# Last image's sums and norms spread by matrix products, x kept in its frame, squares summed by contiguous quarters

## The chip, the cores and the metric

One core of a Trainium2 chip runs the whole program, once, for a batch of 32 images. The metric is the device time in microseconds; runs of the kernel before took 4459.23, 4460.05 and 4460.9 us.

## The reference

The input is 32 images of 128 channels by 64 x 64 positions (T = 4096 tokens of 128 channels), all in float32. Cut to what matters:

```python
# layer 0
x = x + conv(group_norm(x))                  # 3x3 kernels mixed per image by a softmax over 4
# layer 1
t = tokens(x)
t = t + attn(ln_t(t))
t = t + ffn(ln_t(t))
return from_tokens(t)

def attn(x):
    xb  = x @ w_down.T + b_down              # 128 -> 16
    att = windowed_attention(xb)             # 4 heads of 4, windows of 144 tokens at stride 72:
                                             # softmax(q k / 2) v, overlaps added, divided by counts
    out = x + sigmoid(gate) * (att @ w_up.T + b_up)
    return layer_norm(out) * ln_gamma + ln_beta
def ffn(x):
    wx = x @ W.T; wx = batch_norm(wx)        # over all images and tokens
    y_t = sigmoid(wx_t + y_{t-1} @ V.T)      # a scan over the tokens
    return y
```

Three norms over the 128 channels of each token matter here: `ln_t` before the attention (called k = 0 in the kernel), the attention's own layer norm (k = 1), and `ln_t` before the ffn (k = 2). Channels lie on partitions, so the mean and the sum of squares of a token are sums over partitions, and 1/deviation must be brought back to all partitions.

## The kernel before, in words

The program has two stages. `images()` handles the 32 images (b = 0 to 31) as jobs that overlap; `by_runs()` then does the ffn's scan in four streams of two-image groups, which needs the batch norm's statistics of all images and so cannot start before the last image is done.

**Jobs and order.** Each image has thirteen generators (line 1386 on): `load` (statistics, kernel mix), `taps`, `waves`, `conv`, `drain` (a Winograd-like convolution, two halves of 32 rows), `project` (k = 0 norm and projection), `feed`, `values`, `attend` (21 score steps: 7 blocks of windows times 3), `divide0` and `divide1` (softmax denominators, output projection, in two halves of blocks 0 to 3 and 4 to 6), `tail` (k = 1 norm, output x) and `last` (k = 2 norm, ffn input z). Each yields a step: engine, a pool for a result tile, what it reads and writes. A planner that runs when the program is built keeps a model of the five engines (`Clock`), takes the step that can start earliest in the model, and breaks ties by a priority of job and progress from the table `DUE`:

```python
a, w, n = DUE.get(job[0], (-1.0, 0.0, 1))
key = at, job[1] + a + w * job[4] / n - (9 if len(job[3]) > 4 else 0)
```

So each engine's instructions stand in one fixed order, which the table sets. Where the model sees PE idle for over 0.6 us, it puts filler products in (`nm<-fWc`, the constants `SPARE`).

**Tiles.** PSUM: three banks `nms`, one per product of nearly all jobs, given back when the result is read; one four-bank tile `scs` for the scores and for the output projection `wc`; one bank `av` for the weighted values. SBUF: two image frames `xs` (66 x 66 positions, the second stage's first group reuses them as `framed`), three big tiles `zt`, five buffers `places`.

**The norms.** `deviations(src, b, k, mean)` squares the source in four strided parts on ACT into a `place`, sums each over the partitions on PE into one `nm` tile (with the mean beside it for k = 0 and 2), copies that to SBUF, moves it by small DMAs to a tile `cp` of 128 partitions by 32 tokens, takes 1/deviation there (`inv_dev`: exp of -ln/2 and a Newton step), and stores it to `r_d` in DRAM. `spread` then loads each quarter of 1024 tokens from `r_d` to all partitions (512 KB) and multiplies on DVE. In `tail` a second set of loads brings x back from `x_d`, where `project` had stored it.

**The softmax sums.** In `attend` the sums of the exponentials come out as four extra rows in each group of 32 of `av`, copied to `avs` block by block. `divide` moves these rows to `cd` by DMA, takes reciprocals, stores them to `s_d`, loads them spread over the rows, multiplies, loads the mean from `r_d` into row 16 (so that the product with `wc` also subtracts it), and does the products with `wc` and the additions into `zt`.

**The end.** `by_runs` begins with the batch norm's sums (line 1865 on), then loads the z of the next groups. Its group 0 is read from `framed`, which holds the z of images 0 and 1; both were loaded when image 31's k = 0 norm had been applied.

Nearly all instructions of the first stage carry line 243, the planner's recording wrapper, so they are told apart by tile names: `nm`, `sc`, `av` in PSUM, `frames` for `xs`, `place`, `cp`, `cd`, `avs`, `zt`. Parts of names after `<-` are what an instruction reads.

Of the kernel before, what the change touches and what calls it, by code (L numbers as in the profile page):

```python
# [8 lines left out]
F32 = mybir.dt.float32  # L9
AF = mybir.ActivationFunctionType  # L10
ALU = mybir.AluOpType
# [31 lines left out]
    "setup": (0.44, 0.04, 8),  # L43
    "load": (-0.91, 0.63, 29),
    "taps": (0.04, 0.16, 6),
    "waves": (-0.12, 0.52, 26),
# [3 lines left out]
    "feed": (1.63, 0.54, 27),  # L50
    "values": (1.44, 1.24, 28),
    "attend": (1.24, 1.1, 71),
    "divide0": (1.88, 0.1, 15),
    "divide1": (2.21, 0.02, 11),
    "tail": (2.42, 0.75, 33),
    "last": (2.99, 0.86, 40),
# [202 lines left out]
def hybrid_kernel(  # L259
# [60 lines left out]
    )  # L320
    grp = const.tile([P, 32, 4], F32, name="grp")
# [96 lines left out]
    def images(nc):  # L418
# [6 lines left out]
        with ExitStack() as pa:  # L425
# [88 lines left out]
            def deviations(src, b, k, mean):  # L514

                dims = "p (c r y) w -> p r c y w" if k == 0 else "p (c r t) -> p r c t"
                parts = src.rearrange(dims, c=4, r=4)
                for r in range(4):
                    buf = yield from place("ACT", (src,))
                    sq = units(buf)  # L520
                    nc.scalar.activation(
                        sq if k else sq.rearrange("p c (y w) -> p c y w", w=W), parts[:, r], AF.Square
                    )
                    if r == 0:
                        yield "PE", nms, (sq, parts[:, :, :])
                        ps = clock.take("PE", nms)
                    else:
                        yield "PE", None, (sq,)
                    if mean and r == 0:
                        for i in range(4):  # L530
                            for c in range(4):
                                nc.tensor.matmul(
                                    ps[32 * c : 32 * c + 32, UNIT : 2 * UNIT],
                                    avg[:, 32 - i : 64 - i],
                                    parts[:, i, c],
                                    start=(i == 0),
                                    stop=(i == 3),
                                )
                    for c in range(4):
                        nc.tensor.matmul(  # L540
                            ps[32 * c : 32 * c + 32, 0:UNIT],
# [303 lines left out]
            def project(b):  # L845
# [19 lines left out]
                if b == NB - 1:  # L865

                    while ("tail", NI - 1) not in done:
                        yield
# [1269 lines left out]
```

## Time and profile before

| | |
|---|---|
| three runs, median | 4460.05 us (4459.23 to 4460.9) |
| the profiled execution | 4460.42 us, its span 4458.6 us |
| PE busy | 4180.4 us, 94% |
| DVE busy | 3554.4 us, 80% |
| ACT busy | 2410.3 us, 54% |
| POOL busy | 1691.4 us, 38% |
| first stage ends (last `bn_aggr` of image 31) | 3908.6 us |
| mean granted PE clock | 0.975 |

Times in the answers are microseconds from the start of the span. A row of the timeline has start, length, engine, line, operation, tile written, tiles read, shapes and count; in brackets the idle time of the engine before it and what ended that. An fp32 product shows as two PE rows. SPq is the queue of SP, which issues the DMAs; the length of its row is the issue, not the transfer.

### The profile page before, as it was taken

The page shows a single profiled execution, that of the slowest core. Times are in us where ns is not written, and L with a number is a line of the kernel's source. Part 1 is how long each engine was busy: PE and PEld are TensorE (multiplying, and loading weights), DVE is VectorE, ACT ScalarE, POOL GpSimd, SP SyncE. Part 2 cuts the span into 40 slices and gives each one's busy share as a digit, 9 for nine tenths or more (in the row PEclk, how much of TensorE's full clock was granted, in tenths as well). Part 3 has the DMA queues.
Part 4 walks back from the last instruction along what each step waited for, and adds up shares of the span by engine and source line. Part 5 has one row for each costly group of instructions (what it writes and reads, how often), then busy time and mean ns, then how long its engine had stood idle before and what let it go on. Part 6 is the DMA issues. An engine that isn't in the chain of part 4 may idle for free.

```text
span 4458.6 us, 103741 instructions
## 1 busy us (share of the span) xinstructions
PE 4180.4 (94%) x42729; PEld 2191.2 (49%) x42729; DVE 3554.4 (80%) x5364; ACT 2410.3 (54%) x3500; POOL 1691.4 (38%) x1652
## 2 busy tenths in 40 slices
PE   5999999999999999999999999999999998689987
PEld 2544444555455455455455455455455455455443
DVE  7778787888788888888888888888888864459884
ACT  1445555555555555555555555555555565257774
POOL 3443333334334333333333333333333322037765
PEclk9999999999999999999999999999999999899998
DMA  3434554555555555555555555555555544549998
GB/s 105 135 107 168 167 174 146 185 183 174 183 176 172 177 181 177 175 183 164 182 184 171 164 186 168 174 180 172 169 182 179 176 150 148 180 202 264 283 263 171
DMA packets 467575, 789.44 MB, mean 177 GB/s; under 512 B 338048, under 2 KB 348304, under 8 KB 434320
## 3 DMA queue, kind: packets, MB, share of 16 engines
q1 hardware_dynamic: 456480, 715.38, 49.0%
q0 software_dynamic: 8704, 67.11, 7.3%
q8 instruction: 339, 5.55, 0.5%
q14 instruction: 148, 1.21, 0.1%
q10 hardware_dynamic: 1904, 0.18, 0.0%
HBM read 499.06 MB, written 276.76 MB: 174 GB/s over the span
## 4 chain that ended last, share of the span: by engine, by line
PE 61%; DVE 20%; DMA 9%; issue 4%; ACT 2%; SPq 2%; POOL 1%; DVEq 0%; ACTq 0%; POOLq 0%
PE nm L243 33%; PE sc L243 13%; PE av L243 10%; DVE zt L243 6%; PE v L1968 3%; DVE v L1974 3%; DVE frames L243 2%; DMA zr<-z_d 2%; DVE cp L243 2%; SPq L243 2%; ACT ex L243 2%; DMA out_dram<-zr 2%; DVE h L243 1%; DVE st L243 1%; DMA place<-x_d 1%
## 5 line engine op out<-in xcount | busy, mean ns | idle before, releaser
L243 ACT ACTIVATE ex<-sc 128x1728 f32<-128x1728 f32 x672 | 1082.1, 1610 | 825.3 <-PE sc L243 792.9
L243 POOL TENSOR_TENSOR qe<-qs,mqk 128x576 f32<-128x576 f32 x448 | 615.8, 1378 | 1025.1 <-PE sc L243 1020.9
L243 PE MATMUL nm<-u,w 128*128 128x512 f32 x1536 | 785.5, 631 | 19.0 <-POOL w L243 18.9
L243 PE MATMUL sc<-qe,ks 32*128 32x432 f32 (+1 forms) x7168 | 669.6, 443 | 41.9 <-POOL qe L243 21.6
L243 PE MATMUL av<-ex,VE 128*32 128x144 f32 x14336 | 624.6, 292 | 5.7 <-DVE avs L243 5.4
L243 PEld LDWEIGHTS av<-ex,VE 128*32 128x32 f32 x14336 | 390.3, 110 | 313.9 <-issue 244.2
L243 PEld LDWEIGHTS sc<-qe,ks 32*128 32x128 f32 x7168 | 286.2, 185 | 431.0 <-issue 172.1
L1968 PE MATMUL v<-yw,fVT 128*128 128x254 f32 (+1 forms) x1504 | 438.3, 429 | 35.3 <-ACT yw L1981 25.6
L1979 ACT ACTIVATE yw<-v,shf 128x254 f32<-128x254 f32 (+1 forms) x752 | 353.8, 473 | 123.4 <-DVE v L1974 48.2
L1974 DVE SCALAR_TENSOR_TENSOR v<-zr,scl,v 128x256 f32<-128x256 f32 (+1 forms) x585 | 347.5, 662 | 90.5 <-PE v L1968 90.4
L243 PEld LDWEIGHTS nm<-u,w 128*128 128x128 f32 x1536 | 266.3, 194 | 307.4 <-issue 271.7
L243 POOL TENSOR_TENSOR u<-frames 128x528 f32<-128x528 f32 x256 | 392.8, 1544 | 37.1 <-PE nm L243 34.5
L243 PE MATMUL nm<-u,h 128*128 128x512 f32 x768 | 383.4, 618 | 0.0
L1968 PEld LDWEIGHTS v<-yw,fVT 128*128 128x128 f32 x1504 | 242.0, 195 | 244.3 <-ACT yw L1979 194.2
L243 ACT ACTIVATE place<-zt 128x1024 f32<-128x1024 f32 x256 | 259.8, 1050 | 175.9 <-DVE zt L243 166.6
L243 DVE SCALAR_TENSOR_TENSOR u<-u,u 128x528 f32<-128x528 f32 x256 | 246.4, 974 | 58.0 <-POOL u L243 56.5
L1985 POOL COPY zr<-yw 128x256 f32<-128x256 f32 x416 | 257.7, 730 | 85.6 <-ACT yw L1979 84.6
L243 PE MATMUL nm<-zt,fWc 128*128 128x512 f32 x512 | 276.2, 638 | 14.3 <-ACT zt L243 14.2
L243 PE MATMUL nm<-place,avg 128*32 128x256 f32 x3072 | 236.3, 390 | 6.4 <-ACT place L243 6.4
L243 DVE SCALAR_TENSOR_TENSOR zt<-sc,gbk,zt 128x576 f32<-128x576 f32 (+1 forms) x192 | 174.5, 909 | 70.0 <-PE sc L243 69.0
L243 DVE TENSOR_TENSOR zt<-frames,place 128x1024 f32<-128x1024 f32 x128 | 211.5, 1682 | 21.2 <-DMA place<-r_d 21.2
L243 ACT COPY zt<-nm 128x512 f32<-128x512 f32 x256 | 149.1, 584 | 141.0 <-PE nm L243 139.7
(205 smaller groups left out, 6262.7 us busy)
## 6 DMA issues: line engine op xcount, KB each, us to landing
place<-r_d SPq DMA_DIRECT2D x384, 512.0 KB
place<-in_conv_k_dram SPq DMA_DIRECT2D x128, 576.0 KB
x_d<-frames SPq DMA_DIRECT2D x32, 2112.0 KB
place<-x_d SPq DMA_DIRECT2D x128, 528.0 KB
frames<-in_x_dram SPq DMA_DIRECT2D x128, 512.0 KB
out_dram<-zt SPq DMA_DIRECT2D x64, 1024.0 KB
z_d<-zt SPq DMA_DIRECT2D x64, 1024.0 KB
zr<-z_d SPq DMA_DIRECT2D x26, 2048.0 KB
```

What stands on the lines that cost most here:

```text
L243: got = f(*args, **kw)
L1968: nc.tensor.matmul(self.ps[:, :, c], fVT, self.yw[1 - r % 2][:, :, c], start=not whole, stop=True)
L1974: nc.vector.scalar_tensor_tensor(v, z, scl, v, ALU.mult, ALU.add)
L1979: nc.scalar.activation(y[:, :, c], self.ps[:, :, c], AF.Sigmoid, bias=shf)
L1985: nc.gpsimd.tensor_copy(z, y)
```

## The change

For all images, `deviations` takes four contiguous quarters of 1024 tokens, not four strided parts, and each quarter waits only for a gate of its own: for k = 0 the half of the convolution that writes its rows, for k = 2 that quarter of `tail`'s result. The `nm` tile is taken at the first quarter. For the last image alone:

- 1/deviation for k = 1 and 2 is taken on the PSUM sums directly, 128 partitions by 256 tokens (`inv_dev` into a `place`), and `beam` spreads it to all partitions by four products of 32 rows for each quarter, into halves of `scs`; DVE multiplies from PSUM.
- `finish` replaces `divide0` and `divide1`: after each block it spreads the sums by a product with a selector, takes reciprocals of 128 x 288 on DVE and multiplies; the output projection (`added`, split from `divide`) follows after blocks 3 and 6. The mean of k = 0 is subtracted in `project` (`less`).
- x is not stored to `x_d`: ACT adds `bet` to it in its frame, and `tail` adds it from there. Of the first group's z, only the other frame's image is loaded early; this frame's is loaded after `tail` has read x.
- `last` writes its product to a tile of its own, `zw`, so both halves of the product can come ahead of the spread.

The table `DUE` has new values for most jobs. The diff, cut:

```diff
 DUE = {
-    "setup": (0.44, 0.04, 8),
+    "setup": (-0.16, 0.04, 8),
     "load": (-0.91, 0.63, 29),
-    "taps": (0.04, 0.16, 6),
-    "waves": (-0.12, 0.52, 26),
+    "taps": (0.02, 0.22, 6),
+    "waves": (-0.25, 0.4, 26),
     "conv": (-0.45, 1.09, 36),
...
-    "feed": (1.63, 0.54, 27),
+    "feed": (1.72, 0.61, 27),
     "values": (1.44, 1.24, 28),
-    "attend": (1.24, 1.1, 71),
-    "divide0": (1.88, 0.1, 15),
-    "divide1": (2.21, 0.02, 11),
-    "tail": (2.42, 0.75, 33),
-    "last": (2.99, 0.86, 40),
+    "attend": (1.15, 1.27, 71),
+    "divide0": (1.92, 0.02, 15),
+    "divide1": (2.34, 0.02, 11),
+    "tail": (2.39, 0.56, 33),
+    "last": (2.96, 0.89, 40),
 }
...
+            def deviations(src, b, k, mean, gate):
+
+                dims = "p (g j) (v t) -> p j v g t" if k == 0 else "p (g j v t) -> p j v g t"
+                for c in range(4):
+                    while gate(c) not in done:
+                        yield
+                    quart = src[:, 16 * c : 16 * c + 16] if k == 0 else src[:, quarter(c)]
+                    buf = yield from place("ACT", (quart,))
...
+                    nc.scalar.activation(lines(buf[:, 0:QT]) if k == 0 else buf[:, 0:QT], quart, AF.Square)
+                    if c == 0:
+                        yield "PE", nms, (buf[:, 0:QT], quart)
                         ps = clock.take("PE", nms)
...
+                if b == NB - 1 and k:
+                    buf = yield from place("ACT", (ps,))
+                    v, l, dst = (buf[:, UNIT * i : UNIT * (i + 1)] for i in range(3))
+                    if mean:
+                        nc.scalar.activation(l, ps[:, UNIT : 2 * UNIT], AF.Square)
+                        yield "DVE", None, (l, ps), (v,)
+                        nc.vector.tensor_max(v, ps[:, 0:UNIT], l)
+                        nc.vector.tensor_sub(v, v, l)
+                    else:
+                        v = ps[:, 0:UNIT]
+                    yield from inv_dev(dst, v, l)
+                    nms.append(ps)
+                    return buf, dst
...
-                nc.sync.dma_start(
-                    r_d[b, k, n - 2 : 2].rearrange("k (p t) -> p k t", t=32), cp[:, n:4]
-                )
+                for i in range(n, 4):
+                    nc.sync.dma_start(
+                        r_d[b, k, i - 2].rearrange("(g r t) -> r g t", r=4, t=32), cp[:, i]
+                    )
...
+            def beam(got, use):
+
+                buf, dev = got
+
+                def cast(c):
+                    for r in range(4):
+                        nc.tensor.matmul(
+                            ps[:, r, UNIT * (c % 2) : UNIT * (c % 2 + 1)],
+                            once[32 * r : 32 * r + 32, c : c + 1].to_broadcast([32, P]),
+                            dev[32 * r : 32 * r + 32],
+                            start=True,
+                            stop=True,
+                        )
+
+                yield "PE", scs, (dev,)
+                ps = clock.take("PE", scs)
+                cast(0)
+                for c in range(4):
+                    if c < 3:
+                        yield "PE", None, (dev,), (ps[:, :, UNIT * ((c + 1) % 2) : UNIT * ((c + 1) % 2 + 1)],)
+                        cast(c + 1)
+                    yield "DVE", None, (ps,), ()
+                    use(c, ps[:, :, UNIT * (c % 2) : UNIT * (c % 2 + 1)].rearrange("p r (g t) -> p r g t", t=32))
+                scs.append(ps)
+                spare.append(buf)
...
                             nc.vector.scalar_tensor_tensor(y[3], tl, 8.0, y[3], ALU.mult, ALU.add)
+                    done["rows", b, 2 * i] = done["rows", b, 2 * i + 1] = True
...
-                yield "SP", None, (rows(xt, 0, H),)
-                nc.sync.dma_start(x_d[b], xt[:, 1 : H + 1])
-                yield from deviations(rows(xt, 0, H), b, 0, True)
+                if b < NB - 1:
+                    yield "SP", None, (rows(xt, 0, H),)
+                    nc.sync.dma_start(x_d[b], xt[:, 1 : H + 1])
+                yield from deviations(rows(xt, 0, H), b, 0, True, lambda c: ("rows", b, c))
...
+                    yield from spread(less(i) for i in range(4))
+                    yield "ACT", None, (), (rows(xt, 0, H),)
+                    nc.scalar.activation(rows(xt, 0, H), rows(xt, 0, H), AF.Identity, bias=bet)
                     while ("tail", NI - 1) not in done:
                         yield
                     yield "SP", None, ()
-                    for i in range(NI):
-                        nc.sync.dma_start(framed[:, i], z_d[i])
+                    i = (b + 1) % NI
+                    nc.sync.dma_start(framed[:, i], z_d[i])
...
+            def finish(b):
...
+                for m in range(NWG):
+                    while ("block", b, m) not in done:
+                        yield
+                    t = slice(2 * WIN * m, 2 * WIN * (m + 1))
+                    yield "PE", nms, (av[:, t], sel[:, 0:P])
+                    ps = clock.take("PE", nms)
+                    nc.tensor.matmul(ps[:, 0 : 2 * WIN], sel[:, 0:P], av[:, t], start=True, stop=True)
+                    yield "DVE", None, (ps,), (av[:, t], rc)
+                    nc.vector.reciprocal(rc, ps[:, 0 : 2 * WIN])
+                    nc.vector.tensor_mul(av[:, t], av[:, t], rc)
+                    nms.append(ps)
+                    if m in (3, NWG - 1):
+                        yield from added(b, m // 4, zt, DK)
+                spare.append(sel)
...
+                def straight(i, w):
+                    z = zt[:, quarter(i)]
+                    zu = z.rearrange("p (g r t) -> p r g t", r=4, t=32)
+                    nc.vector.tensor_mul(zu, zu, w)
+                    nc.vector.scalar_tensor_tensor(
+                        lines(z), lines(z), gam, rows(xs[b % NF], 16 * i, 16), ALU.mult, ALU.add
+                    )
+                    done["x2", b, i] = True
+
+                got = yield from deviations(zt[:, 0:T], b, 1, False, lambda c: ("div", b, 1))
+                if b < NB - 1:
+                    yield from spread(second(i, k) for i in range(4) for k in range(2))
+                else:
+                    yield from beam(got, straight)
+                    yield "SP", None, (rows(xs[b % NF], 0, H),)
+                    nc.sync.dma_start(framed[:, b % NI], z_d[b % NI])
...
+                got = yield from deviations(zt[:, 0:T], b, 2, True, lambda c: ("x2", b, c))
                 st = sml.tile([P, NBLK, 6], F32, name="st3")
+                zw = zt
+                if b == NB - 1:
+                    zw = big.tile([P, T + 8], F32, name="zt")
+                    for h in range(2):
+                        yield from product(h)
+                    yield from beam(got, straight)
```

## The prediction

> **What bounds the kernel now.** I read the busy times by stage first, then the drain in order of time, then its waits. Stages (stretch in us, its length, then busy us of PE, PEld, DVE, ACT, POOL with instructions, granted PE clock, DMA share, GB/s):
>
> ```profile
> 1000.00:2000.00 1000.00, 973.25 (x11000) 499.51 (x10992) 838.71 (x1224) 545.54 (x724) 362.20 (x291) 0.99 0.56 177
> 2000.00:3000.00 1000.00, 975.95 (x10982) 503.97 (x10984) 848.04 (x1230) 552.25 (x740) 373.68 (x297) 0.99 0.55 175
> ...
> 3728.00:3798.00 70.00, 65.23 (x992) 40.58 (x992) 28.38 (x43) 44.72 (x50) 13.76 (x12) 1.00 0.33 105
> 3798.00:3838.00 40.00, 28.30 (x212) 17.65 (x204) 21.61 (x33) 7.75 (x12) 0.00 (x0) 0.83 0.41 144
> 3838.00:3870.00 32.00, 25.57 (x190) 18.95 (x190) 20.48 (x25) 6.48 (x11) 0.00 (x0) 0.87 0.72 265
> 3870.00:3909.00 39.00, 15.38 (x74) 6.37 (x74) 11.98 (x21) 10.69 (x16) 0.00 (x0) 0.68 0.36 126
> ```
>
> In the steady part PE is busy 97%; 35 us of each 1000 are filler products (`nm<-fWc`, 242 of them in 2000 to 3000). The 32 stores of x to `x_d` start from 89.3 to 3624.5, so an image takes 3535.2/31 = 114.0 us, of which PE has 2.9 idle and 4.0 of filler: 6.9 us of slack. DVE is next, at 84%. From 3798.2, where the last image's attention ends, to 3908.6, where its last `bn_aggr` ends, 110.4 us pass in which no engine is the bound; half of PE's rows are filler. What the time is spent on, in order of time:
>
> ```profile
> 3812.82 0.33 SPq L243 DMA_DIRECT2D s_d<-cd  x1
> ...
> 3821.46 1.06 DVE L243 TENSOR_TENSOR avs<-avs,place 128x864 f32<-128x864 f32 x1 [8.67 <-DMA place<-s_d]
> ...
> 3829.41 1.82 PE L243 MATMUL sc<-avs,wc 17*128 17x432 f32 x8
> ...
> 3877.36 5.36 SPq L243 DMA_DIRECT2D cp<-place  x8
> 3883.96 0.64 DVE L243 TENSOR_TENSOR cp<-cp 128x32 f32<-128x32 f32 x3 [13.54 <-DMA cp<-place]
> ...
> 3886.14 0.33 SPq L243 DMA_DIRECT2D r_d<-cp  x1
> ...
> 3891.66 1.23 DVE L243 TENSOR_TENSOR zt<-zt,place 128x1024 f32<-128x1024 f32 x1 [5.54 <-DMA place<-r_d]
> ...
> 3903.22 1.23 DVE L243 TENSOR_TENSOR zt<-zt,place 128x1024 f32<-128x1024 f32 x1 [6.57 <-DMA place<-r_d]
> ```
>
> Each spread of a small result over the partitions is a chain of transfers: 6.6 us from the issue of `cp<-place` to its first reader, 5.5 from `r_d<-cp` to the first quarter that uses it, and 31 us from the last attention product to the first `wc` product of the second half.
>
> **The last image, step by step** (times are of this execution, 3798.2 onwards; where an operation has no row, the nearest is scaled).
>
> *Softmax sums.* `finish` replaces both `divide(31, d)`: their `cd`, `s_d`, `place` and `avs` transfers go. Added per block: one 128x288 product, a reciprocal and a multiplication. Reciprocals take 0.82 us at 108 and 1.04 at 144 columns, 6.0 ns a column, so 1.9 at 288; the product scales from 128x432 (two rows of 0.54) to 0.7; copy and multiplication 0.45 each. Six of the seven blocks lie in the stretch 3728 to 3798, where DVE is 41% busy: their 6 x 2.4 = 14 us are hidden there; with the cover gone they would cost that. Queued on DVE behind a waiting reciprocal are the spread multiplications of image 30. The last block is on the path: with hops 3.9 us. The selector needs two POOL copies (0.7 us at 256 columns by `zr<-yw`, POOL 20% busy there) and keeps one of five `place` buffers through the attention: nothing while image 30 needs three.
> The four `wc` steps of the first half come out of the transfers' shadow: they now use the one `sc` tile between score steps. Their pitch is 2.7 us (3800.08, 3802.78, 3805.49, 3808.20), together 10.9. A score step already waits for its exponential (21 steps in 70 us, 3.3 each), so the cost lies between 0 and 10.9; I take all of it, because the tile is single. The second half's two steps keep their 8.3 us (3829.41 to 3837.65). Sum: 3798.2 + 10.9 + 3.9 + 8.3 = 3821.3, against 3837.6.
>
> *First norm (tail).* Squares and products keep 4.7 us (3837.32 to 3842.0): 3826.0. Instead of copy, four `cp` transfers, `inv_dev` on 32 columns, `r_d` and broadcasts: `inv_dev` on 256 columns straight from PSUM. It took 1.5 us (3846.93 to 3848.40); two ACT steps grow by 0.19 (0.83 ns a column, from the 256- and 512-column copies), four DVE steps by 0.23 (1.03 ns a column): 2.8 us. The first `cast`, four 32-row products of 256 columns, is between nothing and the 1.0 us of four score products of 432 columns; 0.8 with its hop. Then four quarters of 1.22 + 1.28 = 2.5 us on DVE: 3826.0 + 2.8 + 0.8 + 10.0 = 3839.6, against 3870.4. x comes from its frame, so the last image's store to `x_d` and four loads of 528 KB go. Image 30's last quarters (four of 1.22 + 1.29 us, now at 3837 to 3855) want the same DVE: 0 to 10 us, I take 6: 3845.6.
>
> *Second norm (last).* The squares follow quarter by quarter, so one square (1.05) and its 8 products (1.3) remain behind the last quarter; `inv_dev` with the mean 4.2 (Square, max, sub at 0.42 each, with a hop, on top of 2.8); cast 0.8; four quarters of 1.22 + 1.29 = 10.0; `bn_aggr` 0.4. That is 17.7: **3863.3, against 3908.6, 45.3 us less**. The eight `fWc` products and their copies (0.93 and 0.59 us each) run beside `inv_dev` and the quarters; alone they would take 7.4. Both z stores now start at the end, 1 MB more ahead of the scan's loads: at the 385 GB/s of 3909 to 3950, 2.5 us lost (0 to 3).
>
> *Moved and added upstream.* `less`: four 512 KB loads on SP and four subtractions of 1.2 us, and one ACT pass of about 4 us, in the projection of image 31. Its feed ended at 3704 and its attention could start only at 3727.9 (after `wc` steps of image 30), so 24 us of slack cover these; without it about 9. The load of z into the last frame waits for the frame's last reader and goes ahead of image 31's output stores on SP, which wait for the same quarters. Its 2 MB need 5.4 us at 385 GB/s plus landing; its first use comes some 25 us later. Nothing; 8 uncovered.
>
> *All images.* The same squares and products, cut otherwise; one more DMA issue of 0.33 us for k = 0 on an SP queue with gaps. The new table shifts priorities only. At the start, image 0's squares need not wait for its whole convolution: three squares, 3.1 us, may leave the path, or up to 8 us of setup's small DVE steps come in its way; I take 2 us gained. For the steady period no row prices an order: with all waits of PE on other engines gone (about 90 us in 200 to 3560) 3 us an image would be won; losses are in the rival below. I take 0, within 0.5 us an image.
>
> Sum: 45.3 - 2.5 + 2.0 = 44.8 us from the profiled run's 4460.4 (its span 4458.6; the median is 4460.05): 4415.6, given as 4416.
>
> **Two rules weighed.** In the trace a product into `sc` starts only when DVE has read it (idle 0.62 us, released by `DVE zt`, at 3802.78), so I let each later cast wait for the first step of a quarter and hide under the second (1.28 us): nothing. The Trainium skill ("PSUM — Partial Sum Buffer", section "PSUM bank collisions raise a hardware error") asks to guard by bank and quadrant, not by address, so the cast's two halves of a bank are no real double buffer. If all six later casts were exposed, 6 x 0.8 = 4.8 us would come back: 4420.
> The granted clock fell to 0.68 where PE idled (3870 to 3909), and `nm<-zt,avg` took 0.60 us there against 0.38. I keep full-clock prices since DVE paces the quarters. "TensorE: Matmul & The Clock Gate" (section "Part 1: The HAM clock gate") puts an idle array at half clock; by that the casts and `fWc` products would add an estimated 5 us.
>
> **Rivals.**
> *A bank held too long (slower).* `deviations` takes its `nm` tile at the first quarter and returns it after the fourth. In before, the k = 0 tile is held about 10 us (squares from 2119.13, copy at 2128.09). With the gates, quarter 0 of that image is ready after its half convolution at 2078.2: held 50 us. For k = 2 it grows from 6 to about 22 us (first quarter done at 2086.2, copy at 2107.1). That is 56 of 3 x 114 bank-us in each image, and for most of that time the convolution, the feed and the projections share two tiles of three. For it: PE is at 97%, and no row shows a run with two. Against it: 6.9 us of slack, and products drain in 1 to 3 us. It decides from 44.8/31 = 1.4 us an image; at 2.3 us, a third of the slack, 71 us are lost: 4487.
> *Image 30 sets the end.* `last(31)` starts after `last(30)`, which ended at 3855.4. If nothing speeds it up: 3855.4 + 4.7 + 1.3 + 4.2 + 0.8 + 10.0 + 0.4 = 3876.8, a gain of 32; with 0.5 us an image lost, 4444.
> *The new order wins too.* 0.7 us an image, a quarter of PE's waits, on top: 22 us, 4394; with the `wc` steps hidden, 4383.
> *The transfers were hidden anyway.* Against it: DVE waited 16.6, 15.2 and 8.7 us for them after 3798. I give it no chance of its own.
>
> **How the numbers follow.** Forecast (4395 to 4440): 0.56. Image 30 or small losses (4440 to 4451): 0.14. Order wins: 0.10. Bank held: 0.16. Losses that just cancel the gain: 0.04. A measurement of this kernel can tell about 0.2%, 9 us, from no change. Faster 0.80, same 0.04, slower 0.16. The range runs from 4380 (drain at its best bound, 62 us, and some order) to 4465, leaving out about 0.05 below and 0.14 above. The likeliest case alone: 4395 to 4440.
>
> **What would show it.** Right: period of 114.0 us within 0.5; attention of image 31 ends near 3809; `RECIPROCAL` of 288 columns near 1.9 us; no `s_d`, `x_d` or `cp` rows of image 31 after it; quarters of image 31 at 2.5 us; last `bn_aggr` near 3861; the scan's length within 5 us of 550. Wrong: period over 115.4 us with PE idle before `nm` products, or image 30's `bn_aggr` still near 3855 with DVE idle before image 31's squares.

## The result and the profile after

The changed kernel takes 4438.18 us (median of five runs, 4428.07 to 4441.48) against 4460.05 us: a ratio of 0.9946, 95% interval 0.9931 to 0.9961. Run again later beside other kernels it gave 0.9935 (0.992 to 0.995). The forecast was 4416 us with a range of 4380 to 4465: the sign and the range held, and the gain was about half of the 45 us expected.

The profiled execution is the fastest of the five: 4428.07 us, span 4426.3. Its stages, in the columns of the table before (stretch, length, busy us of PE, PEld, DVE, ACT, POOL with instructions, granted PE clock, DMA share, GB/s):

```profile
1000.00:2000.00 1000.00, 966.76 (x10981) 493.29 (x10984) 840.47 (x1237) 553.14 (x742) 360.75 (x292) 1.00 0.56 179
...
3728.00:3798.00 70.00, 65.02 (x839) 40.44 (x837) 44.56 (x62) 36.25 (x43) 13.26 (x12) 1.00 0.37 116
3798.00:3838.00 40.00, 36.72 (x448) 21.84 (x446) 25.80 (x36) 20.93 (x24) 2.37 (x2) 1.00 0.35 122
3838.00:3870.00 32.00, 28.53 (x225) 16.25 (x228) 22.60 (x30) 13.28 (x21) 0.00 (x0) 1.00 0.58 207
3870.00:3909.00 39.00, 25.07 (x81) 14.25 (x82) 13.39 (x32) 13.73 (x26) 0.00 (x0) 0.82 0.85 352
```

The steady part is nearly as it was: PE 967 us of 1000, where it had 973. In 3728 to 3838 DVE has 70 us of work where it had 50, PE is at full clock, and the images' work ends inside the last row, which is already the scan's loads (352 GB/s). The last image in order of time (start, length, engine, line, operation, tile written, tiles read, shapes, count; in brackets the idle time before and its releaser):

```profile
3714.82 0.29 DVE L243 TENSOR_TENSOR VT<-nm,mvt 128x128 f32<-128x128 f32 x1 [0.23 <-ACT Vc L243]
...
3720.52 1.28 DVE L243 SCALAR_TENSOR_TENSOR zt<-zt,bet,place 128x1024 f32<-128x1024 f32 x1 [0.45 <-DMA place<-x_d]
3721.72 0.18 DVE L243 TENSOR_SCALAR avs<-avs 32x72 f32<-32x72 f32 x1
3721.96 1.34 PE L243 MATMUL sc<-avs,wc 17*128 17x288 f32 x8 [2.55 <-DVE avs L243]
...
3736.07 0.75 DVE L243 TENSOR_TENSOR zt<-zt,sc 128x576 f32<-128x576 f32 x1
...
3736.97 1.01 PE L243 MATMUL sc<-qe,ks 32*128 32x432 f32 x8 [0.51 <-DVE cp L243]
...
3822.22 0.46 DVE L243 COPY avs<-av 128x288 f32<-128x288 f32 x1 [3.19 <-PE av L243]
3823.74 1.96 DVE L243 RECIPROCAL place<-nm 128x288 f32<-128x288 f32 x1 [1.05 <-PE nm L243]
...
3833.94 0.25 DVE L243 TENSOR_SCALAR zt<-zt,gbc 128x64 f32<-128x64 f32 x1
...
3842.79 1.22 DVE L243 TENSOR_TENSOR zt<-zt,sc 128x1024 f32<-128x1024 f32 x1 [1.27 <-PE sc L243]
...
3857.62 0.37 DVE L243 BATCH_NORM_AGGREGATE bnmv<-st 128x2 f32<-128x48 f32 x1
3857.91 0.36 DVE L243 TENSOR_TENSOR place<-nm,place 128x256 f32<-128x256 f32 x1
...
3860.31 4.56 PE L243 MATMUL nm<-zt,fWc 128*128 128x512 f32 x10 [0.85 <-ACT zt L243]
...
3864.80 1.14 PE L243 MATMUL sc<-place,once 32*128 32x256 f32 x16
...
3866.13 1.22 DVE L243 TENSOR_TENSOR zt<-zt,sc 128x1024 f32<-128x1024 f32 x1 [4.65 <-PE sc L243]
...
3876.03 0.37 DVE L243 BATCH_NORM_AGGREGATE bnmv<-st 128x2 f32<-128x48 f32 x1
```

The waits of 13.54, 5.54 and 6.57 us for transfers are gone; the first quarter of the first norm waits 1.27 us for its cast, that of the second 4.65, because the cast stood on PE behind the products with `fWc`. The last `bn_aggr` ends at 3876.4 instead of 3908.6, 32.2 us earlier. The scan is untouched (546.1 us from the copy `bma<-bnmv` to the end in both kernels). Image 31's attention starts late: at 3736.97, behind the first half of image 30's output projection, whose scaling of `avs` stood on DVE behind image 29's last quarters (3721.72). Its own inputs were ready long before: the last of them, `VT`, ends at 3715.1, 21.9 us ahead. Image 30's last `bn_aggr` (3857.62) stands just ahead of the second norm's `inv_dev` (3857.91).

Because executions differ in how long the 31 images before take, the runs are compared by marks counted from image 31's own load (its `bn_aggr` into `mv`). In us; "steady" is the time of that load itself. The last column is a length, from the projection's end to the last `bn_aggr`, in which both norms lie:

| kernel | steady | attention starts | last block copied | projection ends | first quarter of norm k = 1 | `bma` copy (scan starts) | both norms |
|---|---|---|---|---|---|---|---|
| before | 3494.6 | 233.4 | 303.7 | 343.0 | 361.1 | 417.8 | 71.0 |
| changed | 3498.1 | 238.9 | 324.2 | 335.9 | 344.7 | 382.1 | 42.5 |
| sums by transfers | 3506.3 | 220.3 | 296.1 | 337.2 | 345.7 | 380.5 | 39.5 |
| norms by transfers | 3502.5 | 234.4 | 322.4 | 332.8 | 354.8 | 406.9 | 70.4 |
| both by transfers | 3499.1 | 239.7 | 311.5 | 349.9 | 365.2 | 414.5 | 60.9 |
| wc after the last block | 3512.0 | 240.7 | 313.0 | 334.0 | 342.3 | 379.7 | 41.9 |
| wc of image 30 first | 3511.1 | 230.0 | 316.6 | 327.7 | 340.0 | 377.3 | 45.8 |
| no fillers at the end | 3504.9 | 230.4 | 324.1 | 336.2 | 345.1 | 382.9 | 42.9 |

So the stretch after the last load, the drain, is 35.7 us shorter (417.8 to 382.1), and the steady part of this execution 3.5 us longer. The last column is the cleanest measure of the norms: with products it is 39.5 to 45.8 us in all ten profiles of this document (also 44.2 in the changed kernel run once more, 44.1 with the products with `fWc` early, 45.0 with the old table, 45.8 without the gates, 43.6 with one entry moved), with transfers 60.9 to 71.0 in all four (66.2 in the kernel before with the new table), whatever the order.

### The profile page after: what moved, and what is told of

Read it like the earlier page. It is cut to its first block, busy times and chain, and to the rows that moved or that the text cites. A ratio compares the mean times of both kernels' runs of the same rounds, so it can differ in the third digit from the quotient of the medians.

```text
span 4426.3 us, 103608 instructions
## 1 busy us (share of the span) xinstructions
PE 4148.8 (94%) x42643; PEld 2157.1 (49%) x42643; DVE 3550.3 (80%) x5378; ACT 2424.4 (55%) x3500; POOL 1685.1 (38%) x1654
## 5 line engine op out<-in xcount | busy, mean ns | idle before, releaser
L243 PE MATMUL nm<-u,w 128*128 128x512 f32 x1536 | 775.0, 623 | 14.6 <-POOL w L243 12.9
L243 PE MATMUL nm<-u,h 128*128 128x512 f32 x768 | 398.7, 625 | 0.0
L2084 PEld LDWEIGHTS v<-yw,fVT 128*128 128x128 f32 x1504 | 240.7, 194 | 245.6 <-ACT yw L2095 194.3
L243 DVE SCALAR_TENSOR_TENSOR u<-u,u 128x528 f32<-128x528 f32 x256 | 232.0, 920 | 28.1 <-POOL u L243 26.2
L243 POOL TENSOR_TENSOR kt<-ks,mqk 128x384 f32<-128x384 f32 (+1 forms) x96 | 88.4, 920 | 388.7 <-ACT ks L243 333.3
L243 DVE COPY avs<-av 128x288 f32<-128x288 f32 x224 | 100.9, 450 | 164.6 <-PE av L243 163.9
```

The costliest lines, as they stand in the source:

```text
L243: got = f(*args, **kw)
L2084: nc.tensor.matmul(self.ps[:, :, c], fVT, self.yw[1 - r % 2][:, :, c], start=not whole, stop=True)
```

## The experiments

My theory: the gain is the transfers taken out of the last image's chain. Rivals: the table or the quarters for all images made it; held banks cost the steady part what the drain wins; image 30 sets the end.

**The changed kernel once more** (only a comment added).

> The changed kernel once more. Theory: the gain is the drain of the last image (32 us in the profiled execution: the last bn_aggr moved from 3908.6 to 3876.4), and the executions near 4439 lose their extra 10 us in the steady part, by the granted clock. Then the time lies at 4428 to 4441, and in this profile the drain from the end of image 31's attention to the last bn_aggr is 54 us whatever the total. Rival: the drain or the scan itself differs between executions; then this profile has a longer drain or a scan longer than 546 us.

Measured: 4435.04 us (4425.06 to 4438.95). The profiled run's load of image 31 comes at 3498.7 and its drain is 382.3 us, against 3498.1 and 382.1; from the copy of the last block to the last `bn_aggr` it takes 55.9 us, against 54.2. Both profiles are of quick executions, so they do not show where the ones near 4439 lose. The mean granted clocks of the six executions go the way the theory says: 0.985 in the one of 4425.06 us, 0.979 to 0.980 in the three of 4438.43 to 4438.95.

**The changed kernel with the table of before.**

```diff
 DUE = {
-    "setup": (-0.16, 0.04, 8),
+    "setup": (0.44, 0.04, 8),
...
-    "attend": (1.15, 1.27, 71),
+    "attend": (1.24, 1.1, 71),
...
```

> The changed kernel with the priority table of before. Theory (the gain is the drain's own; the table is worth nothing in the steady part): within 10 us of the changed kernel, 4428 to 4450. Rival (the gates hold a PSUM tile too long, and the new table pays for it): the steady part is slower by 0.5 us or more an image, so 4455 or above.

Measured: 4481.96 us, ratio 1.004 (1.0028 to 1.0053): slower than before, in the rival's range. The load of image 31 comes at 3537.9, 113.3 us an image against 112.1; the drain is 396.3.

**The kernel before with only the new table.** The edit is the table in the other direction.

> The kernel before with only the new priority table. Theory: 4450 to 4470, since the table does not touch the drain's transfers. Rival (the new order wins in the steady part on its own): below 4448.

Measured: 4545.77 us, ratio 1.0203 (1.0179 to 1.0226): 114.2 us an image, drain 428.7. Neither range of the expectation holds: the new table alone is worth nothing; it loses 84 us.

**The changed kernel without the gates**, so that the quarters of k = 0 and k = 2 wait for the last one:

```diff
-                yield from deviations(rows(xt, 0, H), b, 0, True, lambda c: ("rows", b, c))
+                yield from deviations(rows(xt, 0, H), b, 0, True, lambda c: ("rows", b, 3))
...
-                got = yield from deviations(zt[:, 0:T], b, 2, True, lambda c: ("x2", b, c))
+                got = yield from deviations(zt[:, 0:T], b, 2, True, lambda c: ("x2", b, 3))
```

> The changed kernel with every quarter's square of k = 0 and k = 2 waiting for the last quarter's gate, so that the PSUM tile is held about 10 us and not 50. Rival (bank held): the steady part gains 0.3 us or more an image, 4425 or below. Theory (the hold costs nothing at 6.9 us of slack): steady part the same within 10 us, and the drain 3 to 6 us longer since the last image's squares come late: 4435 to 4450.

Measured: 4523.44 us, ratio 1.014 (1.0122 to 1.0158): 115.5 us an image, in neither range of the expectation. The drain is 369.1, the shortest of all, 13.0 us shorter than the changed kernel's: in this order image 31's attention starts 217.7 us after its load, 21.2 earlier. These three would say that gates cost 1.4 us an image with one table and bring 3.4 with the other. That is no price of gates, as the last experiment shows.

**Softmax sums and mean of image 31 by transfers** (`divide` for all images, `less` gone, the mean's load back in `tail`; the norms stay products).

```diff
-                    ("divide0", divide(b, 0) if b < NB - 1 else finish(b)),
-                    ("divide1", divide(b, 1) if b < NB - 1 else None), ("attend", attend(b)),
+                    ("divide0", divide(b, 0)),
+                    ("divide1", divide(b, 1)), ("attend", attend(b)),
```

> The changed kernel, with the last image's norm sums and mean taken by the old way: each half of image 31's squares leaves through transfers, and the mean of the squared norms comes back by a transfer too. The spread of x2 by products, x kept in its frame and the attention's and gates' new order stay. Theory (the gain in the drain is the transfers that the products replaced): the prediction put the second divide's way at about 15 us and the mean's return at about 6 us against 5 to 8 us for the products, so the sums and the mean should cost 10 to 20 us, in the stretch between the last attention and the last statistics alone: 4448 to 4458 us. Rival (the drain is shorter because the attention of image 31 starts on a freer chip and the transfers were hidden): within 4 us of the changed kernel, 4434 to 4442 us.

The expectation speaks of norm sums and of squares; what the edit undoes are the softmax sums and the mean of k = 0. Measured: 4439.46 us (4434.77 to 4451.05), ratio 0.9969 (0.9957 to 0.9981), drain 380.5. By the medians (4438.18 and 4435.04 for the changed kernel) the products for the sums bring 1 to 4 us, by the drain nothing; by the ratios up to 15. My theory is wrong for this part. Its trace shows what became of them:

```profile
3802.45 0.45 DVE L243 COPY avs<-av 128x288 f32<-128x288 f32 x1
...
3830.18 1.06 DVE L243 TENSOR_TENSOR avs<-avs,place 128x864 f32<-128x864 f32 x1 [7.28 <-DMA place<-s_d]
...
3852.04 1.22 DVE L243 TENSOR_TENSOR zt<-zt,sc 128x1024 f32<-128x1024 f32 x1 [1.27 <-PE sc L243]
```

The transfers are there and take 41 us from the last block to the end of the projection (12 with products). But the last block is copied 28.0 us earlier: the attention starts 18.6 us earlier and is 9.4 shorter. DVE does image 30's quarters while `s_d` is under way (of the 28 us between the first two rows it idles 15), and the projection ends within 1.4 us of where it ends in the changed kernel.

**Norms of image 31 by transfers** (the sums stay products; x not kept in its frame).

```diff
-                if b == NB - 1 and k:
+                if False:
                     buf = yield from place("ACT", (ps,))
```

> The changed kernel, with image 31's second deviations stored and loaded back as in the kernel before (x in its frame undone as well), while the sums and the mean still come by products. Theory: the second step's products, casts and quarters, about 11 us from the cast of x2 to the last statistics, are replaced by a store, a load and a pass over the loaded tile, so 10 to 25 us come back behind the last attention: 4448 to 4463 us. Rival (transfers hidden): 4434 to 4442 us. If both this and the run with the sums by transfers cost about half of the 36 us by which the drain became shorter, the two parts add up; if one alone costs it all, the other part is idle.

The expectation counts the second norm alone; the edit undoes both. Measured: 4460.6 us (4448.58 to 4472.23), ratio 1.0009 (0.9997 to 1.002): the whole gain is gone. The drain is 406.9, 24.8 us longer, and the two norms take 70.4 us in place of 42.5. The waits of before are back in its rows:

```profile
3835.26 0.25 DVE L243 TENSOR_SCALAR zt<-zt,gbc 128x64 f32<-128x64 f32 x1
...
3863.74 1.28 DVE L243 SCALAR_TENSOR_TENSOR zt<-zt,bet,place 128x1024 f32<-128x1024 f32 x1 [2.60 <-DMA place<-x_d]
...
3880.29 0.64 DVE L243 TENSOR_TENSOR cp<-cp 128x32 f32<-128x32 f32 x3 [9.09 <-DMA cp<-place]
...
3888.82 1.23 DVE L243 TENSOR_TENSOR zt<-zt,place 128x1024 f32<-128x1024 f32 x1 [6.38 <-DMA place<-r_d]
...
3900.23 1.23 DVE L243 TENSOR_TENSOR zt<-zt,place 128x1024 f32<-128x1024 f32 x1 [6.42 <-DMA place<-r_d]
```

**Both by transfers**, leaving the quarters, the gates and the table.

> The changed kernel with both parts for the last image undone: its softmax sums and mean by transfers, its norms by transfers, x loaded back. What is left of the change is the contiguous quarters with their gates and the new table. From the load of image 31 (its last step cv) to the batch norm's first copy the traces show 413 us before, 379 after, 378 with the sums alone by transfers and 402 with the norms alone by transfers. Theory A (the parts add up: the sums' products are worth 0, the norms' products 24, and the rest, 10, came with the gates and the table): 402 us in this stretch, 4456 to 4466 us in all. Theory B (the sums' products are worth 10 where the norms still go by transfers, and are hidden only beside the norms' products): 411 to 415 us in this stretch, 4466 to 4476 us in all.

Measured: 4460.47 us, ratio 1.0003 (0.9993 to 1.0013); drain 414.5. So quarters, gates and table together are worth nothing, and the norms' products 21 us by the medians (4460.47 to 4439.46) and 34.0 by the drain where the sums go by transfers, 24.8 by the drain where they go by products; in their own stretch 21.4 (60.9 to 39.5) and 27.9 (70.4 to 42.5). The sums' products are worth 7.6 of drain beside norms by transfers, and no time (4460.47 and 4460.6). In this pair the attention did not slide forward (239.7 after the load, 234.4 with the sums' products) and the projection does end 17.1 us earlier with the products (332.8, not 349.9). The other 9.5 us are lost behind it, where with the products image 30 still has 21.7 us to its last `bn_aggr` after the projection's end, and with transfers 2.8; that this is the reason is likely, not shown. Theory B of the expectation described the drain, theory A the time; between the two the 10 us differences of order and execution decide nothing.

**Products with `fWc` early**: each pair as soon as its quarter is squared, in place of all eight ahead of the second cast.

```diff
+                for i in range(NBLK):
+                    while ("x2", b, i // 2) not in done:
+                        yield
...
+                    nc.tensor.matmul(ps, fWc, zt[:, s], start=True, stop=True)
```

> The changed kernel, with image 31's eight products with fWc moved out of the place just before the second spread: each pair starts as soon as its quarter of the squares is done. In the changed kernel's trace the second spread's first cast waited about 3.3 us behind these eight products on TensorE, and the prediction had put them beside it at no cost. Theory (that wait is on the path to the end): 2.5 to 3.5 us less, 4434 to 4436 us beside 4438. Rival (DVE's last step is held by image 30's statistics or by the mean's inverse, so what is taken off TensorE is waited for there): less than 1 us, 4437 to 4439 us. Second rival: the products' evictions on ACT delay the casts of the first spread, 1 to 4 us slower.

Measured: 4440.02 us, ratio 0.9954 (0.9941 to 0.9967); drain 381.5, 0.6 us shorter: the first rival's case by the drain, though the median lies 2 to 5 us above the changed kernel's two. The norms take 44.1 us, against 42.5 and 44.2 in the changed kernel's two profiles. The wait went and came back one step earlier:

```profile
3879.55 0.42 DVE L244 TENSOR_TENSOR place<-nm,place 128x256 f32<-128x256 f32 x1 [4.77 <-ACT place L244]
...
3884.51 1.22 DVE L244 TENSOR_TENSOR zt<-zt,sc 128x1024 f32<-128x1024 f32 x1 [1.32 <-PE sc L244]
```

The first quarter waits 1.32 us for its cast, not 4.65, but DVE had waited 4.77 for the sums, whose squares now queue on ACT behind the copies of these products.

**No fillers after the last convolution.**

```diff
-                if job[3][0] == "PE" and "setup" in done:
+                if job[3][0] == "PE" and "setup" in done and ("conv", NB - 1) not in done:
```

> The changed kernel without filler products after the last convolution is done. In its trace fillers stood on TensorE ahead of image 31's attention (24 of them in 4.36 us at half the clock) and the attention started 9 us later than in the kernel before and lasted 85 us. Theory A (fillers delay the attention): the attention of image 31 starts 4 to 9 us earlier and the drain is that much shorter: 4429 to 4434 us. Theory B (fillers hold the clock in gaps that nothing else fills): the granted clock in the stretch from the last convolution to the last statistics falls below the 1.00 of the changed kernel, its products double in length, and the drain becomes 5 to 25 us longer: 4443 to 4463 us.

Measured: 4432.6 us, ratio 0.9951 (0.9938 to 0.9964); drain 382.9, 0.8 us longer. Neither theory: the attention starts 8.5 us earlier, as A said, but lasts 93.7 us in place of 85.2; the clock falls, as B said, and the end does not move.

```profile
3798.00:3838.00 40.00, 29.23 (x298) 13.80 (x287) 26.79 (x37) 15.11 (x20) 1.31 (x1) 0.81 0.31 104
3838.00:3870.00 32.00, 22.94 (x144) 7.75 (x141) 20.02 (x28) 12.00 (x17) 0.00 (x0) 0.60 0.32 113
```

```profile
3847.83 2.09 PE L243 MATMUL sc<-place,once 32*128 32x256 f32 x16 [2.89 <-DVE place L243]
3850.01 1.22 DVE L243 TENSOR_TENSOR zt<-zt,sc 128x1024 f32<-128x1024 f32 x1 [2.24 <-PE sc L243]
...
3856.07 1.22 DVE L243 TENSOR_TENSOR zt<-zt,sc 128x1024 f32<-128x1024 f32 x1 [0.94 <-PE sc L243]
...
3873.45 1.22 DVE L243 TENSOR_TENSOR zt<-zt,sc 128x1024 f32<-128x1024 f32 x1 [5.93 <-PE sc L243]
...
3878.62 1.22 DVE L243 TENSOR_TENSOR zt<-zt,sc 128x1024 f32<-128x1024 f32 x1 [0.18 <-PE sc L243]
```

That the end stays is a sum of moves, not a clock without effect. In these rows DVE waits 9.3 us for casts (2.24, 0.94, 5.93 and 0.18), in the changed kernel 5.9 (1.27 and 4.65): 3.4 us more. The stretch of the norms is only 0.4 longer (42.9) because image 30 is out of its way: its last `bn_aggr` comes 2.7 us after the projection's end, not 23.7.

**Image 31's output projection after its last block**, not after blocks 3 and 6.

```diff
-                    if m in (3, NWG - 1):
-                        yield from added(b, m // 4, zt, DK)
+                    if m == NWG - 1:
+                        yield from added(b, 0, zt, DK)
+                        yield from added(b, 1, zt, DK)
```

> The changed kernel with both halves of image 31's output projection after its last block, so that no wc step stands between its score steps. The prediction charged 10.9 us for the four steps among the score steps, because they share the one sc tile, and the trace shows an attention of 85 us in place of 70. Theory A (they cost the attention what they take, and can stand nowhere better): the attention is 11 to 15 us shorter and the projection after it 11 us longer, so the time stays within 3 us of the changed kernel, 4432 to 4441 us. Theory B (among the score steps they cost more than their own 10.9, since each blocks the tile while DVE works for image 30): 3 to 8 us less, 4430 to 4435 us. Theory C (they were partly hidden there): 3 to 10 us more, 4441 to 4448 us.

Measured: 4435.06 us, ratio 0.9939 (0.9925 to 0.9952). Theory A: from its start to the last block the attention takes 72.3 us, not 85.2, so the four steps cost it 13 us, and the projection is 9 us longer after it. The drain is 379.7, 2.4 shorter.

**Image 30's projection steps ahead of image 29's quarters.**

```diff
+                    if job[0] == "divide0" and job[1] == NB - 2:
+                        at += -3.0
```

> The changed kernel, in which the planner takes the steps of image 30's first output projection as if they could start 3 us earlier, so that they stand ahead of image 29's last quarters on DVE. In the trace of the changed kernel these quarters (eight steps of 1.3 to 1.9 us, 3707 to 3722) stood ahead of them, and image 31's attention, which waits for them, started 9 us later than before. Theory A (the late start of the attention sets the end): the attention starts 7 to 15 us earlier and the end comes as much earlier, 4423 to 4431 us. Theory B (DVE has the work of images 29 and 30 to do in any order, and it comes back ahead of the last norms): less than 3 us, 4435 to 4441 us. The run with the sums by transfers speaks for B: its attention ended 18 us earlier and its first quarter with 1/deviation started no earlier.

Measured: 4436.98 us, ratio 0.9943 (0.993 to 0.9957): no faster than the changed kernel, as theory B has it; by the drain, 4.8 us shorter, it lies between the two. The attention starts 8.9 us earlier and its projection ends 8.1 earlier. Much of the rest goes to a transfer for image 30, queued on DVE ahead of image 31's `inv_dev`:

```profile
3843.14 1.23 DVE L243 TENSOR_TENSOR zt<-zt,place 128x1024 f32<-128x1024 f32 x1 [4.05 <-DMA place<-r_d]
```

**One entry of the table moved by 0.02.**

```diff
-    "attend": (1.15, 1.27, 71),
+    "attend": (1.17, 1.27, 71),
```

> The changed kernel with one entry of the table DUE moved by 0.02 (attend's first value 1.15 to 1.17, so that every image's attention stands 0.02 of an image later among equals). Nothing else differs, but the planner's order differs from image 2 on. The runs so far show the steady part, from the first load to image 31's, at 112.1 us an image in the changed kernel (111.9 to 112.7 over nine executions of this one order), 113.3 with the old table, 115.5 without the gates, and 114.2 for the kernel before with the new table. Theory A (a table is fitted to one kernel, and any step off it costs 1 to 3 us an image, so these losses say nothing of the gates and of held banks): 113 to 115 us an image, 4465 to 4530 us. Theory B (the steady part feels the table little near its values, and the losses above are what the gates and the cuts cost or bring): 111.6 to 112.8 us an image, 4425 to 4455 us.

Measured: 4494.47 us (4490.0 to 4498.72), ratio 1.0077 (1.006 to 1.0094): 34 us slower than before. The load of image 31, the last of 32 (least, middle and greatest duration in ns, first and last start), in the changed kernel and in this one:

```profile
L243 DVE BATCH_NORM_AGGREGATE mv<-st x32: 371/372/373, 23.4 to 3498.1; 128x2 f32<-128x48 f32 x32
```

```profile
L243 DVE BATCH_NORM_AGGREGATE mv<-st x32: 371/372/373, 23.3 to 3537.8; 128x2 f32<-128x48 f32 x32
```

39.7 us later, 1.3 an image, and the drain is 405.0, 22.8 longer, 21.7 of it ahead of the projection's end (357.6 after the load, not 335.9). Theory A, for the one step that was tried: it costs 1.3 us an image, so the losses with the old table, with the new one alone and without gates (1.2 to 3.4 an image) cannot be read as the price of the table or of the gates. It also says how far a drain can be trusted: a change of order alone moves it by over 20 us, so differences of a few us between drains are no price either. The length of the two norms hardly moved (43.6).

## Why the prediction was right, and where it was not

**Right: the norms by products.** From the projection's end to the last `bn_aggr` I had 42.0 us (3821.3 to 3863.3) against 71.0 before. Measured: 3833.94 to 3876.4, 42.5. `inv_dev` on 256 columns took 2.7 (2.8), the quarters 2.46 each (2.5), `inv_dev` with the mean 5.1 (4.2), 1.2 of it behind image 30's last rows. Two terms inside cancelled. The products with `fWc` did not run beside: they held the second norm's first cast 3.3 us. Image 30 took less than the 6 us: its first two quarters fitted into the wait for the sums, its last two delayed the second `inv_dev` by about 3 (5.2 us from the last quarter to it, 2.4 in the run with the sums by transfers, where image 30 was done before). The runs put this part at 21 to 34 us by medians and drains (15 by the ratios in the pair with the sums by transfers) and at 21 to 28 us by the norms' own stretch; my 29 is at the upper end.

**Wrong: the softmax sums, 16.3 us.** Counted from the load, the projection ends 7.1 us earlier than before, and the runs give the sums' products between -1.6 and 7.6 us of drain and 0 to 4 us by the medians (up to 15 by the ratios). The failed step is the start of that sum: I took the attention's end, 3798.2, as given and added the four `wc` steps. In the trace the last block is copied at 324.2 us after the load instead of 303.7, 20.5 later where I had 10.9: the start moved by 5.5 (9 by the clock of the two executions, as the expectations above have it), which I had at nothing, and the length by 15.0, not 10.9. The 24 us of slack for the work moved upstream did hold: image 31's inputs are ready 21.9 us before its attention starts. What moved the start is image 30's output projection, which stands ahead of it on the `sc` tile and came later in the new order. The experiments add that correcting this one term would not have mended the sum. In the runs that share the changed kernel's order up to image 31's load, an attention that starts 8.5 to 18.6 us earlier or is 13 us shorter brought 4.8 us at most. Why is argued, not shown: DVE and the `sc` tile have images 29, 30 and 31 to finish between 3728 and 3838, but no engine is full there (DVE 70 of 110 us; of PE's 102, 28 are fillers), and in the wholly different order without the gates a start 21.2 us earlier goes with a drain 13.0 shorter. With the sums by transfers, the beginning of the chain of 31 us slid forward into them in one run (the attention 18.6 us earlier) and not in the other (239.7), where the products do end the projection 17.1 us earlier, close to my 16.3, and 7.6 reach the end. So the waits that I listed before (8.67 us ahead of `avs`) were real, and what taking them away is worth depends on what the order puts around them.

**Right by luck: the steady part.** I said 0 within 0.5 us an image, "the new table shifts priorities only". On the mean the sum is right: nine executions that share the changed kernel's order up to image 31 load it at 3498.1 to 3517.1, mean 3505.5, against 3494.6 in the one profiled execution of before: 0.1 to 0.7 us an image, 0.35 on the mean, which is 10.9 us in all. The reason is wrong: priorities alone are worth over 1 us an image. The table and the gates were each dear without the other, but so is a step of 0.02. The held banks are not settled: products into `nm` waited more (45.3 us in all against 11.0), as some of these rows of PE's waits in 1000 to 3400 show (us in total, times, longest), first of the changed kernel, then of before,

```profile
PE nm L243 <- DVE h L243: 21.4, 13, 2.4
...
PE nm L243 <- ACT place L243: 8.0, 19, 1.0
PE nm L243 <- ACT qs L243: 5.7, 8, 0.8
```

```profile
PE nm L243 <- DVE frames L243: 7.1, 19, 0.7
...
PE nm L243 <- DVE VT L243: 3.6, 7, 0.6
```

but whether a held bank or the new order makes them wait was not tried.

**The account of the 22.6 us** from 4415.6 to the median of 4438.2: 9.6 in the drain (45.3 less 35.7, all of it before the attention's end), 5.5 in the steady part of the profiled execution (3.5 longer, 2.0 shorter expected), less 2.5 for the scan, which lost nothing, and 10.1 between this execution and the median one. If the later executions lose their time before image 31's load, as the nine profiles suggest, the larger part of the shortfall lies in the steady part and not in the sums.

**The two rules.** The casts after the first pair waited for DVE's read and ran under the second step of each quarter, so none of the 4.8 us came. The first quarter started only after the first two casts, 1.14 us together, where I had 0.8 for one. The Trainium skill ("PSUM — Partial Sum Buffer", section "PSUM bank collisions raise a hardware error") asks that a product and a reader in one bank and quadrant be kept apart, at whatever address; the order here agrees (the two casts end at 3842.72, DVE's read starts at 3842.79), but that it is the cause was not tried. For the clock, the run without fillers is the test: from the projection's end to the last `bn_aggr` the clock was 0.66 instead of 0.98, the first two casts took 2.09 us instead of 1.14, and DVE waited 3.4 us more for casts. "TensorE: Matmul & The Clock Gate" (section "Part 1: The HAM clock gate") states half rate for an idle array, and 2.09 against 1.14 us is near that. In the changed kernel the 5 us estimated from it were not paid, since fillers held the clock at 0.98 in this stretch; without them 3.4 were.

**The rivals.** Image 30 did not set the end: with the sums by transfers its last `bn_aggr` comes 17.1 us earlier after the load than in the changed kernel (342.5, not 359.6) and the drain is 1.6 shorter. The new order did not win. "The transfers were hidden anyway", which I gave no chance, is what happened to the softmax sums in the changed kernel's order.

## What to carry to other kernels

A wait on a transfer is worth its length only if the work ahead of it cannot slide: before counting it, ask whether the chain that feeds it could have started earlier into the same gap, and count the end of a chain (here the norms) in full. For the middle, expect less, and ask what else stands on the same engines and tiles. In a kernel with an order written by a planner, test a change to the order's inputs by a tiny step of one input first: here 0.02 moved the time by 1.3%, so differences of 1% between table variants say nothing of what the edits cost. Count runs from a mark close to the edit, not by the total, and end at one just behind it: here the length of the two norms parted products from transfers in fourteen profiles, while the drain moved by over 20 us with the order alone.

## What the runs showed of the hardware that was not expected

One instruction order, run nine times, reached the same point at 3498.1 to 3517.1 us. The difference grows in steps of a few us at several images, with granted clocks of 0.97 to 1.00 in every 500 us stretch in the quick and the late ones alike. The shares hide a difference, though: by the traces' clock records, 58 to 92 us before that mark stood at half clock, 58 to 65 in the three earliest executions and 89 in the latest (68 in the one at 3512.0, so it is not the whole of it). Whether a lowered clock makes an execution late, or a gap on PE lowers the clock, is open. The scatter is as large as most of the effects asked about here.

Fillers that hold the clock up brought nothing on balance in the drain: without them the clock fell to 0.60 in 3838 to 3870, DVE waited 3.4 us more for casts and the attention took 8.5 us longer, but it started 8.5 earlier and image 30 was done sooner, and the end moved by 0.8 us in 383.
